# Two graph layers on one core: a PSUM bank for each matching tile, one power per tile, small steps back on VectorE, and the first gathers spaced by a GpSimd step

## The chip, the cores and the metric

The kernel runs on one core of a Trainium2 chip. The metric is the device time of one execution in microseconds (us); less is better. The kernel before took 754.28 us, the median of 14 runs (747.26 to 760.17).

## What is computed

`x` is 4096 x 512 and `adj` is 4096 x 4096, both float32. About 0.2% of `adj` is not zero, and the diagonal is always there, so a row has about nine entries. Cut to what matters:

```python
# layer 0
a = adj + eye;  d = a.sum(1) ** -0.5
x = layernorm(x + relu((d[:, None] * a * d[None, :]) @ x @ W.T + b))
# layer 1: eight heads, masked so hard that each row attends to itself alone
x = layernorm(x + einsum(softmax(q k^T / 8 + 0.01 eye - 1e16 (1 - adj)), x @ Wv, Wo))
```

Off the diagonal an entry of `adj` is below one, so the mask leaves every row only itself; layer 1 is then a product with one 512 x 512 matrix, `wvo`. The kernel tests that this holds and goes to a general version (`general`) where it doesn't. With the given data that version is not run.

## The kernel before

**Tiles.** There are 32 row tiles of 128 rows. In `order`, twelve tiles come first, then the five that stay in SBUF, then the rest, which are loaded a second time.

**First phase** (about 0 to 220 us of the profile). All of `adj` is read once. ScalarE sums rows, TensorE computes `y = d * (x @ W.T)`, which goes to DRAM. VectorE already sorts out entries: for each row tile, `extraction` takes the eight largest of every 512 columns with `max` and `max_index` (L731, L732), sixteen long instructions a tile, and packs value and column into `rec` with some twenty-five short ones.

**Second phase** (from about 220 us to the end). For every tile `i` the loop runs `k` from 0 to 9. At each `k` it emits, in this order and for all engines together, one matmul with a 128 x 128 selection matrix `s_t` against a gathered tile `g` (L1265), one gather 18 ahead (`gather`, L1057, an indirect DMA issued by GpSimd; 19 buffers), one build of a later `s_t` by ScalarE (`spread`, L955 to L968), and a share of VectorE's extraction. Ten such products make one tile of layer 0. The rest of a tile's way is spread over the next three tiles' steps by the table `at`: T transposes the result `h` on TensorE and copies it to `hT` (L668), M multiplies by `wvo` (`times`, L675), Q takes squares on ScalarE, V adds them on VectorE, the power -1/2 is taken by GpSimd (`power`, L1164), and F scales and stores on ScalarE (`finish`, L1170). An entry (2, 6) means: at step 6 of the tile that comes two later. `near` is the table of the last two tiles, `far` that of the others. `scaled` and `residual` (L1126, L1137, VectorE) come at step 1 of the next tile, `eps_var` (L1151, ScalarE) at its step 6.

**Matching.** Rows have different numbers of entries, so rows are paired and long ones hand entries to short ones. This is a chain of six stages per tile, each called at a fixed step: KEY (ScalarE, L808) from the row counts `n_all`; ACROSS (TensorE, L815) transposes the key into PSUM; RANKS (ScalarE, L822) reads that; PERM (VectorE, L832); MOVE (TensorE, L840 and L843) writes merged entries to PSUM; END (VectorE, L851 to L854, and ScalarE, L856) reads them into `wr_all` and `cols_all`. Both PSUM results lie in one bank, the tile `bank`: `pk` in columns 0 to 127, `merged` behind it.

**Order.** [...] An instruction that waits holds everything behind it on its engine. [...]

Of the kernel before, what the change touches and what calls it, by code (L numbers as in the profile page):

```python
# [9 lines left out]
FP = mybir.dt.float32  # L10
# [409 lines left out]
def few_edges_below_one(  # L420
# [46 lines left out]
    ps_a = ctx.enter_context(tc.tile_pool(name="ps_a", bufs=5, space=bass.MemoryType.PSUM))  # L467
    first = ExitStack()
    p1 = first.enter_context(tc.tile_pool(name="first", bufs=2))

# [239 lines left out]
    def extraction(t, a_t, rec):  # L710

        v = v_all[:, t, :]
        vu = v.bitcast(U32)
        idx = keys.tile([P, C], U32, name="idx")
        key = keys.tile([P, 2, C], U32, name="key")
        keyf = key.bitcast(FP)
        top = keys.tile([P, 2, K], FP, name="top")  # L720
        topu = top.bitcast(U32)
        own = keys.tile([P, E], FP, name="own")
        mask = keys.tile([P, C], FP, name="mask")
        ints = keys.tile([P, 2, K], U32, name="ints")
        w = rec[:, 1]
        home = slice(t // TS * E, (t // TS + 1) * E)
        long = []
        for s in range(SEGS):
            o = slice(s * E, (s + 1) * E)
            seg = a_t[:, ts(s, SW)]  # L730
            long.append(lambda o=o, seg=seg: nc.vector.max(v[:, o], seg))  # L731
            long.append(lambda o=o, seg=seg: nc.vector.max_index(idx[:, o], v[:, o], seg))  # L732

        def stt(out, a, sc, b, op0, op1, **kw):
            return lambda: nc.vector.scalar_tensor_tensor(out, a, sc, b, op0=op0, op1=op1, **kw)

        def both(a):
            return a.rearrange("p (o c) -> p o c", o=1).to_broadcast([P, 2, a.shape[1]])

        def one(out, a, s1, s2, **kw):  # L740
            return lambda: nc.vector.tensor_scalar(out, a, s1, s2, **kw)

        def top8(f, r):
            return lambda: nc.vector.max(top[:, f, r * 8 : r * 8 + 8], keyf[:, f])  # L744
# [6 lines left out]
        short = [  # L751
            [

                stt(own, idx[:, home], spot[:, t % TS : t % TS + 1], v[:, home],
                    ALU.is_equal, ALU.mult, accum_out=own_all[:, t : t + 1]),
                stt(key[:, 0], idx, 12, place[:, 0], ALU.logical_shift_left, ALU.bitwise_or),
            ],
            [
                stt(key[:, 1], vu, 0x7FFFF, place[:, 1], ALU.bitwise_and, ALU.bitwise_or),
                stt(key[:, 0], vu, 19, key[:, 0], ALU.logical_shift_right, ALU.bitwise_or),  # L760
            ],
            [stt(keyf, both(v), 0.0, keyf, ALU.is_gt, ALU.mult)],
            [stt(keyf[:, :, home], both(own), 0.0, keyf[:, :, home], ALU.is_equal, ALU.mult)],
            [
                top8(1, 0),
                lambda: nc.scalar.activation(
                    mask, keyf[:, 0], AF.Sign, accum_out=n_all[:, t : t + 1]
                ) if second else nc.vector.tensor_scalar(
                    mask, keyf[:, 0], 0.0, 0.0, op0=ALU.is_gt, op1=ALU.add,
                    accum_out=n_all[:, t : t + 1],  # L770
                ),
            ],
            [drop(1, 0), top8(0, 0)],
            [top8(1, 1), drop(0, 0)],
            [drop(1, 1), top8(0, 1)],
            [top8(1, 2), drop(0, 1)],
            [top8(0, 2)],
            [
                one(ints[:, 1], topu[:, 0], 0xFFF, 19, op0=ALU.bitwise_and,
                    op1=ALU.logical_shift_left),  # L780
                one(ints[:, 0], topu[:, 0], 12, 0xFFF, op0=ALU.logical_shift_right,
                    op1=ALU.bitwise_and),
            ],
            [
                stt(w.bitcast(U32), topu[:, 1], 0x7FFFF, ints[:, 1],
                    ALU.bitwise_and, ALU.bitwise_or),
                lambda: nc.vector.tensor_copy(rec[:, 0], ints[:, 0]),
            ],
            [one(rec[:, 2], w, 0.0, row1n, op0=ALU.is_gt, op1=ALU.mult)],
            [lambda: nc.vector.tensor_tensor(  # L790
                rec[:, 3:6], rec[:, 0:3], upper(rec)[:, 0:3], ALU.subtract
            )],
            [lambda: nc.vector.tensor_tensor(
                rec[:, 6], rec[:, 4], upper(rec)[:, 4], ALU.subtract
            )],
        ]
        return long, short


    bank = ps_t.tile([P, 512], FP, name="bank", bufs=1)  # L800
    second = []

    def match_key(t):
# [7 lines left out]
        return key  # L811

    def match_across(key):
        pk = bank[:, :P]
        tc.keep_in_program_order(nc.tensor.transpose(pk, key.to_broadcast([P, P]), ident))  # L815
        return pk

# [17 lines left out]
    def match_move(rec, perm):  # L835

        r = upper(rec)
        merged = bank[:, P : P + 7 * KH].rearrange("p (f k) -> p f k", f=7)
        tc.keep_in_program_order(
            nc.tensor.matmul(merged, perm[:, 0], r[:, :, :KH], start=True, stop=False)  # L840
        )
# [7 lines left out]
    def match_end(t, merged):  # L849
# [2 lines left out]
        nc.vector.tensor_tensor(wr[:, 0:3], wr[:, 0:3], merged[:, 3:6], ALU.add)  # L852
        nc.vector.tensor_tensor(wr[:, 1], wr[:, 1], merged[:, 6], ALU.add)  # L853
        nc.vector.tensor_scalar(cols_all[:, t], wr[:, 0], float(N - 1), None, op0=ALU.min)  # L854
        if second:
            nc.scalar.activation(wr[:, 3], wr[:, 1], AF.Copy, scale=-1.0)  # L856
        else:
            nc.vector.tensor_scalar(wr[:, 3], wr[:, 1], -1.0, None, op0=ALU.mult)

# [186 lines left out]
    mat = ctx.enter_context(tc.tile_pool(name="mats", bufs=3))  # L1046
    AHEAD = 18

    SUMMED = (NT - 2, NT - 1)
    slots = {}  # L1050

    def gather(j):
        if j >= NT * KH:
            return
        t, k = order[j // KH], j % KH
        slots[j] = p2.tile([P, D], FP, name="g", bufs=AHEAD + 1)
        nc.gpsimd.indirect_dma_start(  # L1057
            out=slots[j], out_offset=None, in_=y[:, :],
# [52 lines left out]
    def own_part(i):  # L1111
        t = order[i]
        own = own_all[:, t : t + 1]
        d = d_all[:, t : t + 1]
        nc.scalar.activation(own, own, AF.Identity, scale=d, bias=d)  # L1115

    def own_bias(i):
        own = own_all[:, order[i] : order[i] + 1]
# [10 lines left out]
        )  # L1129

    def residual(i, c=slice(0, D), part=0):
        if i % 2 == 0 and i not in sts:
            sts[i] = small.tile([P, 2, 5], FP, name="sums")
            sts[i + 1] = sts[i][:, 1]
            pairs[i] = sts[i]
            sts[i] = sts[i][:, 0]
        nc.vector.scalar_tensor_tensor(  # L1137
            hs[i][:, c], hs[i][:, c], 0.0, xs[i][:, c], op0=ALU.max, op1=ALU.add,
            accum_out=sts[i][:, part : part + 1],
# [17 lines left out]
            st[:, 3:4], st[:, 3:4], LN_EPS * LN_EPS, st[:, 1:2], op0=ALU.add, op1=ALU.add  # L1157
        )

    def power(i, n):  # L1160

        j = i % 2
        st = pairs[i - j][:, j : j + n]
        nc.gpsimd.tensor_tensor(  # L1164
            st[:, :, 4], st[:, :, 3], mhalf.to_broadcast([P, n]) if n > 1 else mhalf, ALU.pow
        )

    def finish(i):
        r_t = p2.tile([P, D], FP, name="r_t")
# [36 lines left out]
    yo, zs, hs, pts, hTs, ws, sts, pairs, mats, halves = ({} for _ in range(10))  # L1206
# [11 lines left out]
    shares = iter(was + (n + 1) * (count[1] - was) // (SPREAD * KH) for n in range(SPREAD * KH))  # L1218


    def at(step, i, k):

        near = {"T": (1, 5), "M": (1, 8), "Q": (2, 2), "V": (2, 3), "F": (2, 7)}
        far = {"T": (2, 0), "M": (2, 6), "Q": (3, 1), "V": (3, 4), "F": (3, 8)}
        for table, tiles in ((near, range(NT - 2, NT)), (far, range(NT - 2))):
            behind, place = table[step]
            if k == place and i - behind in tiles:
                return i - behind
        return None

    for i in range(NT + 2):
        if i < NT:
# [3 lines left out]
        has_p = 0 <= p < NT  # L1236
        for k in range(KH):
            ends = p == NT - 1
            t = at("T", i, k)
            if t not in (None, NT - 1):  # L1240
                hTs[t] = evacuate(p2, "hT", transpose_rows(hs[t]))
            t = at("M", i, k)
            if t not in (None, NT - 1):
                ws[t] = times(hTs.pop(t), wvo)
            if i == NT - 1:

# [43 lines left out]
                load_own(i + 2)  # L1290
            if k == 3 and i + 1 < NT:
                own_part(i + 1)
            t = at("Q", i, k)
            if t is not None:
                squares(ws[t], D**-0.5, sts[t][:, 3:4])

            t = at("V", i, k)
            if t is not None:
                variance(t)
                if t >= NT - 2:  # L1300
                    power(t, 1)
                elif t % 2:
                    power(t - 1, 2)
            if k == 6 and i < NT:
                own_bias(i)
            if k == 6 and has_p:
                eps_var(p)
            t = at("F", i, k)
            if t is not None and (t >= NT - 2 or t % 2):
                if t < NT - 2:  # L1310
                    finish(t - 1)
# [43 lines left out]
```

## Time and profile before

| | us |
|---|---|
| median of 14 runs | 754.28 |
| the profiled execution, its own time | 759.6 |
| its span, first to last instruction | 757.7 |
| TensorE busy (matmul) | 600.5 |
| VectorE busy | 546.1 |
| ScalarE busy | 525.3 |
| GpSimd busy | 395.1 |

The profiled execution took 759.6 us, of which 757.7 is the span and 1.9 lies around it. It is 5.3 us (0.7%) over the median. Busy times are shares of one execution; matmuls overlap, so a busy TensorE is not one at its peak. In the waits, "A <- B" says that A stood idle until B released it, "issue" that the profile shows no reason, and "remote" that the releaser isn't in the profile. The granted clock is the share of full speed that TensorE got.

### The profile page before, as it was taken

The numbers are of one execution on the slowest core, as the hardware profiler recorded it, in microseconds if no ns is written. First come the engines' busy times: TensorE is split into PE (matmuls) and PEld (weight loads), VectorE is DVE, ScalarE is ACT, GpSimd is POOL, SyncE is SP. The second block draws the span as 40 slices with busy tenths as digits, with TensorE's granted clock in tenths as the row PEclk, the third lists the DMA queues.
The fourth block names the chain that finished last, engine by engine and source line by source line (L and its number), as shares of the span: only waits on it lengthen the run. The fifth ranks groups of instructions, "written<-read, shape, count | busy, mean of one in ns | idle before, by whom it ended". The sixth has DMA issues, their size and how long they took to land. (4 is left out here: it accounts for less than half of the span.)

```text
span 757.7 us, 8023 instructions
## 1 busy us (share of the span) xinstructions
PE 600.5 (79%) x1638; PEld 276.8 (37%) x1638; DVE 546.1 (72%) x2109; ACT 525.3 (69%) x1152; POOL 395.1 (52%) x494
## 2 busy tenths in 40 slices
PE   1799969877816489689888899988977789798592
PEld 0444434333302134244434344433433344343251
DVE  6679989999996298879969999787884343323310
ACT  2787697858875378579868698777853978775222
POOL 3223223322347566667665676675755566767500
PEclk9999989999967789799999999999998799999887
DMA  9999999999947599999998899987986567678501
GB/s 344 403 422 422 422 428 401 424 422 380 422 174 258 169 361 361 327 357 352 389 337 305 296 321 324 367 282 254 357 296 203 171 210 258 213 225 252 186 14 61
DMA packets 54411, 230.54 MB, mean 304 GB/s; under 512 B 8592, under 2 KB 9616, under 8 KB 48080
## 3 DMA queue, kind: packets, MB, share of 16 engines
q1 hardware_dynamic: 18416, 119.55, 40.0%
q0 software_dynamic: 30800, 100.95, 39.1%
q10 hardware_dynamic: 5136, 9.44, 3.3%
q14 instruction: 44, 0.36, 0.1%
q8 instruction: 15, 0.25, 0.1%
HBM read 213.12 MB, written 16.78 MB: 303 GB/s over the span
## 5 line engine op out<-in xcount | busy, mean ns | idle before, releaser
L1057 POOL DMA_INDIRECT g<-y,cols_all x320 | 314.4, 982 | 147.8 <-issue 77.5
L1265 PE MATMUL acc<-g,s_t 128*128 128x512 f32 x600 | 286.5, 624 | 20.0 <-DMA yo<-y 19.3
L731 DVE MAX8 v_all<-a_t 128x8 f32<-128x512 f32 x256 | 169.2, 681 | 17.1 <-DMA a_t<-in_adj_dram 17.1
L732 DVE FIND_INDEX8 idx<-v_all,a_t 128x8 uint32<-128x512 f32 x256 | 174.3, 685 | 0.0
L1265 PEld LDWEIGHTS acc<-g,s_t 128*128 128x128 f32 x600 | 116.3, 201 | 153.5 <-issue 151.0
L675 PE MATMUL acc<-wvo,hT 128*128 128x512 f32 x256 | 130.9, 653 | 28.5 <-ACT hT L668 11.8
L675 PE MATMUL acc<-wT,xT 128*128 128x512 f32 x256 | 123.6, 630 | 16.2 <-ACT xT L668 11.9
L687 ACT ACTIVATE dump<-a_t 128x2048 uint8<-128x2048 f32 (+1 forms) x52 | 119.5, 2298 | 0.8 <-ACT s_t L968 0.8
L675 PEld LDWEIGHTS acc<-wvo,hT 128*128 128x128 f32 x256 | 52.0, 210 | 93.9 <-issue 70.5
L675 PEld LDWEIGHTS acc<-wT,xT 128*128 128x128 f32 x256 | 49.2, 201 | 73.1 <-issue 52.2
L959 ACT ACTIVATE s_t<-sq,wr_all 128x128 f32<-128x128 f32 x160 | 71.9, 484 | 0.3 <-ACT sq L955 0.3
L955 ACT ACTIVATE sq<-cols,wr_all 128x128 f32<-128x128 f32 x192 | 67.0, 392 | 6.6 <-DVE wr_all L851 4.1
L968 ACT ACTIVATE s_t<-s_t,wr_all 128x128 f32<-128x128 f32 x150 | 52.3, 390 | 4.4 <-ACT r_t L1170 2.5
L682 ACT ACTIVATE dump<-a_n 128x4096 uint8<-128x4096 f32 x15 | 54.4, 3630 | 0.3 <-DMA a_n<-in_adj_dram 0.3
L744 DVE MAX8 top<-key 128x8 f32<-128x64 f32 x192 | 39.4, 216 | 19.2 <-remote 14.0
L856 ACT ACTIVATE wr_all<-wr_all 128x10 f32<-128x10 f32 x24 | 5.0, 208 | 57.1 <-DVE wr_all L853 32.0
L694 POOL TENSOR_SCALAR deg<-deg_all 128x1 f32<-128x1 f32 x32 | 6.9, 234 | 64.4 <-ACT dump L682 64.3
L540 POOL DMA_DIRECT2D x_t<-in_x_dram x32 | 18.0, 566 | 42.1 <-PE pt L663 41.7
L1119 DVE SCALAR_TENSOR_TENSOR yo<-yo,own_all,b_bc 128x512 f32<-128x512 f32 x32 | 23.8, 744 | 21.9 <-ACT own_all L1115 8.7
L704 POOL DMA_DIRECT2D y<-y_t x32 | 19.0, 594 | 37.4 <-ACT y_t L702 36.8
L1164 POOL TENSOR_TENSOR sums<-sums,mhalf 128x2 f32<-128x2 f32 (+1 forms) x17 | 12.4, 727 | 49.6 <-DVE sums L1156 45.0
L702 ACT ACTIVATE y_t<-acc,d_all 128x512 f32<-128x512 f32 x32 | 21.5, 686 | 23.1 <-POOL d_all L697 17.8
(123 smaller groups left out, 668.0 us busy)
## 6 DMA issues: line engine op xcount, KB each, us to landing
a_t<-in_adj_dram SPq DMA_DIRECT2D x30, 2048.0 KB
a_n<-in_adj_dram SPq DMA_DIRECT2D x15, 2048.0 KB
x_t<-in_x_dram POOLq DMA_DIRECT2D x32, 256.0 KB
y<-y_t POOLq DMA_DIRECT2D x32, 256.0 KB
yo<-y SPq DMA_DIRECT2D x32, 256.0 KB
x_t<-in_x_dram SPq DMA_DIRECT2D x32, 256.0 KB
out_dram<-r_t ACTq DMA_DIRECT2D x32, 256.0 KB
g<-y,cols_all POOLq DMA_INDIRECT x320
```

Of the source, the lines that this page charges most:

```text
L675: nc.tensor.matmul(u, srcT[:, dc, :], w[:, dc, :], start=(dc == 0), stop=(dc == ND - 1))
L682: nc.scalar.activation(dump[:, : part.shape[1]], part, AF.Copy, accum_out=dst)
L687: nc.scalar.activation(dump[:, o], a_t[:, o], AF.Relu, scale=-1.0, accum_out=neg_all[:, t, halves[0] : halves[0] + 1],)
L731: long.append(lambda o=o, seg=seg: nc.vector.max(v[:, o], seg))
L732: long.append(lambda o=o, seg=seg: nc.vector.max_index(idx[:, o], v[:, o], seg))
L744: return lambda: nc.vector.max(top[:, f, r * 8 : r * 8 + 8], keyf[:, f])
L955: nc.scalar.activation(sq, cols1, AF.Square, bias=wr[:, 2, k : k + 1])
L959: nc.scalar.activation(s_t[:, k, :], away(), AF.Relu, scale=wr[:, 3, k : k + 1], bias=wr[:, 1, k : k + 1],)
L968: nc.scalar.activation(s_t[:, k, :], s_t[:, KH, :], AF.Copy, scale=wr[:, 1, k : k + 1])
L1057: nc.gpsimd.indirect_dma_start(out=slots[j], out_offset=None, in_=y[:, :], in_offset=bass.IndirectOffsetOnAxis(ap=cols_all[:, t, k : k + 1 ...
L1119: nc.vector.scalar_tensor_tensor(yo[i], yo[i], own, b_bc, op0=ALU.mult, op1=ALU.add)
L1265: nc.tensor.matmul(zs[i], mats[i][:, k, :], slots.pop(i * KH + k), start=(k == 0), stop=(k == KH - 1),)
```

## The change

- **PSUM.** `bank` becomes two tiles, `pk` and `pm`, of a bank each. `acc` gets four banks in place of five.
- **From ScalarE to VectorE**, in the second phase: the count of a row's entries (`n_all`, L766), the negated weights at the end of END (L856), and `own_part` (L1115). KEY and RANKS stay on ScalarE.
- **Powers.** `power` and `finish` are called for each tile, not for pairs of tiles; the sums get a tile of 128 x 5 each.
- **Steps.** The copy to `hT` gets a step E of its own, three steps behind the transposes; `eps_var` gets a step S, ten steps behind `residual` in place of five; M, Q, V and F move by one or two steps. The matching is called in another order and at other steps.
- **Spacing.** Ahead of each of the gathers 4 to 39, GpSimd adds one to a 128 x 100 constant and writes it to a tile that nothing reads.

```diff
-    ps_a = ... tile_pool(name="ps_a", bufs=5, PSUM)
+    ps_a = ... tile_pool(name="ps_a", bufs=4, PSUM)
...
-                lambda: nc.scalar.activation(mask, keyf[:, 0], AF.Sign, accum_out=n_all[:, t : t + 1])
-                if second else nc.vector.tensor_scalar(mask, keyf[:, 0], 0.0, 0.0, ...),
+                one(mask, keyf[:, 0], 0.0, 0.0, op0=ALU.is_gt, op1=ALU.add, accum_out=n_all[:, t : t + 1]),
...
-    bank = ps_t.tile([P, 512], FP, name="bank", bufs=1)
-        pk = bank[:, :P]
+        pk = ps_t.tile([P, 512], FP, name="pk", bufs=1)[:, :P]
-        merged = bank[:, P : P + 7 * KH].rearrange("p (f k) -> p f k", f=7)
+        pm = ps_t.tile([P, 512], FP, name="pm", bufs=1)
+        merged = pm[:, : 7 * KH].rearrange("p (f k) -> p f k", f=7)
...
-        if second:
-            nc.scalar.activation(wr[:, 3], wr[:, 1], AF.Copy, scale=-1.0)
-        else:
-            nc.vector.tensor_scalar(wr[:, 3], wr[:, 1], -1.0, None, op0=ALU.mult)
+        nc.vector.tensor_scalar(wr[:, 3], wr[:, 1], -1.0, None, op0=ALU.mult)
...
+    SPACED = range(4, 4 * KH)
+    space = p2.tile([P, 100], FP, name="space", bufs=1)
...
+        if j in SPACED:
+            nc.gpsimd.tensor_scalar(space, cols1[:, :100], 1.0, None, op0=ALU.add)
         slots[j] = p2.tile([P, D], FP, name="g", bufs=AHEAD + 1)
         nc.gpsimd.indirect_dma_start(...)
...
-        nc.scalar.activation(own, own, AF.Identity, scale=d, bias=d)
+        nc.vector.tensor_scalar(own, own, 1.0, d_all[:, t : t + 1], op0=ALU.add, op1=ALU.mult)
...
-    def power(i, n):        # n = 2: a pair of tiles
+    def power(i):
+        st = sts[i]
+        nc.gpsimd.tensor_tensor(st[:, 4:5], st[:, 3:4], mhalf, ALU.pow)
...
-        near = {"T": (1, 5), "M": (1, 8), "Q": (2, 2), "V": (2, 3), "F": (2, 7)}
-        far = {"T": (2, 0), "M": (2, 6), "Q": (3, 1), "V": (3, 4), "F": (3, 8)}
+        near = {"T": (1, 5), "E": (1, 5), "M": (1, 8), "S": (1, 6), "Q": (2, 2), "V": (2, 3), "F": (2, 7)}
+        far = {"T": (2, 0), "E": (2, 3), "M": (2, 7), "S": (2, 1), "Q": (3, 0), "V": (3, 3), "F": (3, 6)}
...
-                match(*{1: (RANKS,), 3: (MOVE, PERM), 6: (END,), 7: (KEY,), 9: (ACROSS,)}.get(k, ()))
+                match(*{2: (RANKS,), 4: (MOVE,), 5: (PERM, KEY), 8: (ACROSS, END)}.get(k, ()))
```

More of the change, by code (lines that the diff above doesn't have):

```diff
@@ L466, in few_edges_below_one @@
     ps_t = ctx.enter_context(tc.tile_pool(name="ps_t", bufs=2, space=bass.MemoryType.PSUM))
-    ps_a = ctx.enter_context(tc.tile_pool(name="ps_a", bufs=5, space=bass.MemoryType.PSUM))
+    ps_a = ctx.enter_context(tc.tile_pool(name="ps_a", bufs=4, space=bass.MemoryType.PSUM))
     first = ExitStack()
@@ L765, in extraction @@
                 top8(1, 0),
[L766 to L771, printed above, removed]
+                one(mask, keyf[:, 0], 0.0, 0.0, op0=ALU.is_gt, op1=ALU.add,
+                    accum_out=n_all[:, t : t + 1]),
             ],
@@ L1113, in own_part @@
         own = own_all[:, t : t + 1]
-        d = d_all[:, t : t + 1]
-        nc.scalar.activation(own, own, AF.Identity, scale=d, bias=d)
+        nc.vector.tensor_scalar(own, own, 1.0, d_all[:, t : t + 1], op0=ALU.add, op1=ALU.mult)
     def own_bias(i):
@@ L1131, in residual @@
     def residual(i, c=slice(0, D), part=0):
[L1132 to L1136, printed above, removed]
+        if i not in sts:
+            sts[i] = small.tile([P, 5], FP, name="sums")
         nc.vector.scalar_tensor_tensor(
@@ L1158, in variance @@
         )
-    def power(i, n):
[L1162 to L1166, printed above, removed]
+    def power(i):
+        st = sts[i]
+        nc.gpsimd.tensor_tensor(st[:, 4:5], st[:, 3:4], mhalf, ALU.pow)
     def finish(i):
@@ L1204, in test @@
         nc.vector.tensor_scalar(bad, both[0:1, :], -1.0, 1.0, op0=ALU.mult, op1=ALU.add)
-    yo, zs, hs, pts, hTs, ws, sts, pairs, mats, halves = ({} for _ in range(10))
+    yo, zs, hs, pts, hTs, ws, sts, mats, halves = ({} for _ in range(9))
     to_build = iter(
@@ L1218, in few_edges_below_one, with at @@
     shares = iter(was + (n + 1) * (count[1] - was) // (SPREAD * KH) for n in range(SPREAD * KH))
-    def at(step, i, k):
-        near = {"T": (1, 5), "M": (1, 8), "Q": (2, 2), "V": (2, 3), "F": (2, 7)}
-        far = {"T": (2, 0), "M": (2, 6), "Q": (3, 1), "V": (3, 4), "F": (3, 8)}
+    def at(step, i, k, end=NT):
+        found = []
+        near = {"T": (1, 5), "E": (1, 5), "M": (1, 8), "S": (1, 6), "Q": (2, 2), "V": (2, 3), "F": (2, 7)}
+        far = {"T": (2, 0), "E": (2, 3), "M": (2, 7), "S": (2, 1), "Q": (3, 0), "V": (3, 3), "F": (3, 6)}
         for table, tiles in ((near, range(NT - 2, NT)), (far, range(NT - 2))):
             behind, place = table[step]
-            if k == place and i - behind in tiles:
-                return i - behind
-        return None
+            if k == place and i - behind in tiles and i - behind < end:
+                found.append(i - behind)
+        return found
     for i in range(NT + 2):
@@ L1238, in few_edges_below_one @@
             ends = p == NT - 1
[L1239 to L1243, printed above, removed]
+            for t in at("T", i, k, NT - 1):
+                pts[t] = transpose_rows(hs[t])
+            for t in at("E", i, k, NT - 1):
+                hTs[t] = evacuate(p2, "hT", pts.pop(t))
+            for t in at("M", i, k, NT - 1):
                 ws[t] = times(hTs.pop(t), wvo)
@@ L1292, in few_edges_below_one @@
                 own_part(i + 1)
-            t = at("Q", i, k)
-            if t is not None:
+            for t in at("Q", i, k):
                 squares(ws[t], D**-0.5, sts[t][:, 3:4])
-            t = at("V", i, k)
-            if t is not None:
+            for t in at("V", i, k):
                 variance(t)
[L1300 to L1303, printed above, removed]
+                power(t)
             if k == 6 and i < NT:
                 own_bias(i)
[L1306 to L1311, printed above, removed]
+            for t in at("S", i, k):
+                eps_var(t)
+            for t in at("F", i, k):
                 finish(t)
```

## The prediction

> **What bounds the kernel now.** I read the page first, then the busy time by windows, the groups of the second phase, and the order of time on VectorE, GpSimd and TensorE. The windows come first (start and end, length, then busy time and count of each engine, clock, DMA share):
>
> ```profile
> 240.00:260.00 20.00, 11.71 (x28) 4.74 (x26) 4.78 (x16) 5.10 (x13) 14.29 (x16) 0.93 0.68 207
> 300.00:320.00 20.00, 12.56 (x25) 4.90 (x25) 15.89 (x58) 11.56 (x33) 13.14 (x14) 0.74 0.92 314
> 340.00:360.00 20.00, 19.39 (x54) 8.66 (x53) 20.00 (x78) 18.23 (x49) 15.11 (x16) 1.00 0.97 349
> 230.00:565.00 335.00, 286.00 (x742) 128.12 (x743) 274.75 (x993) 243.42 (x675) 221.23 (x228) 0.92 0.89 317
> 565.00:745.00 180.00, 151.12 (x400) 69.35 (x398) 61.64 (x244) 110.10 (x308) 100.18 (x106) 0.92 0.61 193
> ```
>
> Where nothing disturbs (340 to 360) TensorE is busy 19.39 of 20 us and a tile takes about 13 us. The 21 tiles from 230 to 565 took 16 us each. TensorE was busy for 437.1 us of the 515 us of phase two; the other 78 us are waits, and they are what this change can reach. From 240 to 260 only GpSimd is at work: VectorE has 4.78 us of work, ScalarE 5.10. VectorE there:
>
> ```profile
> 244.13 0.95 POOL L1057 DMA_INDIRECT g<-y,cols_all  x1 [0.30 <-DMA g<-y,cols_all]
> 246.63 0.94 POOL L1057 DMA_INDIRECT g<-y,cols_all  x1 [0.30 <-issue]
> 248.10 0.17 DVE L735 SCALAR_TENSOR_TENSOR key<-own,key 128x16 f32<-128x16 f32 x1 [3.44 <-issue]
> 252.31 0.23 DVE L744 MAX8 top<-key 128x8 f32<-128x64 f32 x1 [3.42 <-remote]
> 260.69 0.23 DVE L744 MAX8 top<-key 128x8 f32<-128x64 f32 x1 [4.57 <-remote]
> 264.04 0.48 PE L815 MATMUL bank<-ident,rank_key 128*128 128x128 f32 x1 [9.80 <-ACT above L822]
> 281.04 0.95 POOL L1057 DMA_INDIRECT g<-y,cols_all  x1 [0.30 <-issue]
> 295.40 3.60 PE L1265 MATMUL acc<-g,s_t 128*128 128x512 f32 x8
> ```
>
> Each of these instructions is as short as elsewhere; what grows is the wait ahead of it, and VectorE waits for its own earlier instruction. GpSimd meanwhile issues 27 gathers without a break, one per 1.25 us (0.95 and a gap of 0.30). Such waits add up to 50.8 us between 224 and 590, and to 0.6 us between 30 and 224, where there are no gathers. TensorE, in order, ends up behind L815. The groups from 230 us on:
>
> ```profile
> L815 PE MATMUL bank<-ident,rank_key 128*128 128x128 f32 x23 | 7.1, 308 | 32.3 <-DVE wr_all L853 11.3 <-ACT above L822 9.8 <-DVE v_all L731 3.0
> L675 PE MATMUL acc<-wvo,hT 128*128 128x512 f32 x256 | 130.9, 653 | 28.5 <-ACT hT L668 11.8 <-issue 11.6 <-ACT rank_key L808 4.4
> L856 ACT ACTIVATE wr_all<-wr_all 128x10 f32<-128x10 f32 x24 | 5.0, 208 | 57.1 <-DVE wr_all L853 32.0 <-DVE idx L732 8.7 <-DVE v_all L731 6.1
> L1164 POOL TENSOR_TENSOR sums<-sums,mhalf 128x2 f32<-128x2 f32 x15 | 11.2, 750 | 40.2 <-DVE sums L1156 35.5 <-DVE rec L741 3.1 <-issue 1.3
> ```
>
> L815 and L675 hold 60.8 us of TensorE's 78.
>
> **The change part by part**, against the profiled execution (759.6 us: span 757.7, 1.9 around it; 5.3 over the median of 754.28).
>
> *A bank each.* ACROSS (L815, step 9) overwrites the tile that END (step 6) reads, so TensorE stands behind VectorE's L853: 11.3 us in four waits. With two tiles it waits only for its key and the last RANKS; END and the next MOVE are six steps apart. What is late next is T, which waits for `h` from VectorE: 3.5 us now (L663). I take 11.3 - 3.5 = -7.8; bounds 0 and 32.3 - 9.8 = 22.5 (the 9.8 belongs to the spacing). One `acc` bank less costs nothing: a buffer is needed again after four allocations, which is two tiles, while a product tile is freed at step 1 of the next and the `wvo` tile 9 steps after M. If that cover were gone, TensorE would wait for F, about two steps or 2.6 us a tile.
>
> *To VectorE.* ScalarE loses 24 x 0.208 (L856) + 18 x (0.244 + 0.191) (L766) + 31 x 0.380 (L1115) = 24.6 us of work, and the 57.1 us for which L856 held it. Behind L856 stand the builds, the copy to `hT` and KEY, for which TensorE waits 11.8 + 4.4; 5.1 of that is the last tile's, which keeps its steps. Of the other 11.1 I take half, -5.5; bounds 0 and 11.1. VectorE gains about 24 x 0.157 (as L853) + 18 x 0.29 (the first phase's form) + 31 x 0.206 (as L1156) = 15.4 us. It no longer waits for ScalarE's `own_part` (8.7) and mask (8.1), which would pay for it, but not in full windows: 4 of the 17 between 230 and 565 have VectorE at 19.9 of 20 or more. 4/17 of 15.4 is +3.6; bounds -1.4 and 15.4.
>
> *Steps.* `eps_var` moves to ten steps behind `residual`, so ScalarE's 17.7 us behind L1137 go; Q has three steps after M in place of five, so its 12.9 us on TensorE may grow. By count of the stages, END comes one to five tiles ahead of its gathers in both versions. I take 0; bounds -5 and +5, that difference of 4.8 either way.
>
> *Powers.* 32 x 0.558 against 15 x 0.750 + 2 x 0.558 is 5.5 us more on GpSimd, and 15 more gaps of 0.30: 10.0. Gathers queue behind them, and for gathers `gather` runs 18 x 1.25 = 22 us ahead, so 0 on the path; without that cover, 10.0.
>
> *Spacing.* The trace has no such step. A 128x1 tensor_scalar on GpSimd took 0.234 us, the 128x128 select 0.284; an instruction behind a gather started 0.03 us after it. I take 0.30 a step, 36 x 0.30 = 10.8 us on GpSimd, and little else is queued there. The first forty gathers are consumed as they land (3.2 us after their start), so this is on the path: number 4 starts at 227.85 as now, number 40 at 227.85 + 36 x 1.55 = 283.7 in place of 281.04, and it lands at 286.9. Tile 3 could then end at 287.5; it ended at 299.0 (295.40 + 3.60). So if the breaks let VectorE go on, -11.5; if they don't, +2.6. A second stall at 305 to 312 (7.2 us on L675) could go too, so the bounds are -18.7 and +2.6. I take -11.5, since VectorE is slow only within unbroken runs of gathers.
>
> [...]
>
> After the 9.80 wait fourteen halves of products took 8.31 us from 266.61, against 6.17 from 323.13 at full clock. [...]
>
> *Sum.* -7.8 - 5.5 + 3.6 - 11.5 = -21.2: 738.4 against the profiled 759.6, and 733.1 on the scale of the median.
>
> **Rivals.** *The spacing does nothing* (VectorE's slow waits have another cause), the rest works: 754.3 - 7.8 - 5.5 + 3.6 = 744.6. For it: later slow stretches (390 to 397, 545 to 553) also come in runs of only 9 to 11 gathers.
>
> *VectorE takes all back*: no gain from spacing, and 15.4 us wholly on the path: 754.3 - 13.3 + 15.4 = 756.4. For it: VectorE is at 274.75 of 335, and 50 of the rest is slow waits. Against it: the 16.8 us that it no longer waits for ScalarE.
>
> *Slower: powers hold the gathers.* Every power now waits in GpSimd's queue for its own variance, and the spaced gathers have used up the lead. Gathers alone would end at 223.95 + 320 x 1.25 + 10.8 + 32 x 0.86 = 662; the last ends now at 712.8, and 33 us follow. Up to the last gather L1164 waited 18.8 us for L1156, four times, 4.7 each. From 50 us of such waits on GpSimd sets the end. If 16 of 32 wait, 75 us: 662 + 75 + 33 + 1.9 = 772 profiled, 767 as a median. Against it: four of 17 waited, which scaled to 32 is 35 us.
>
> **How the numbers follow.** Forecast 0.42 (733), spacing idle 0.20 (745), VectorE 0.14 (756), powers 0.24 (767). About 0.5% (3.8 us) is what a measurement can tell from no change; so faster 0.62, same 0.14, slower 0.24. The range goes from 714, near the sum with the larger bounds of the bank and the spacing (-22.5 - 5.5 + 3.6 - 18.7 = -43.1, 711), to 767, where the slower case stands.
>
> **What would show it.** Right: between 240 and 260 VectorE is busy 12 us or more; L815 no longer waits for L853, and its idle time falls from 32.3 to under 15; L668 and L808 release L675 for under 10 us; tile 3 ends by 290. Wrong: VectorE's waits for itself stay near 50 us, or only move behind gather 40; L1164 waits over 50 us before the last gather, and L1265 then waits for `g`.

## The result and the profile after

The changed kernel took 769.57 us (median of 10 runs) against 752.92 us for the kernel before (47 runs beside them): 1.0219, with a 95% interval of 1.0184 to 1.0254. It is 16.7 us slower where the forecast was 21.2 us faster. The profiled execution took 772.44 us, its span 770.6. One thing is needed to read the numbers below: in some comparisons the kernel before ran at about 750 us and in others at about 710, so each kernel is held only against the runs of the kernel before that were made beside it.

The windows of the changed kernel (start and end, length, then busy time and count of TensorE, its weight loads, VectorE, ScalarE, GpSimd, then granted clock, DMA share, GB/s):

```profile
240.00:260.00 20.00, 11.80 (x28) 4.16 (x27) 14.23 (x57) 18.22 (x48) 17.71 (x24) 0.84 0.70 243
300.00:320.00 20.00, 12.48 (x32) 5.30 (x30) 7.28 (x31) 4.50 (x10) 13.85 (x15) 0.91 0.84 285
340.00:360.00 20.00, 19.34 (x49) 8.83 (x50) 19.87 (x87) 18.91 (x48) 14.70 (x16) 0.91 0.94 349
230.00:565.00 335.00, 269.07 (x690) 118.25 (x691) 257.33 (x1020) 228.77 (x598) 234.86 (x263) 0.89 0.85 303
565.00:745.00 180.00, 154.41 (x418) 70.18 (x417) 82.77 (x303) 113.07 (x299) 116.18 (x123) 0.95 0.70 226
```

From 240 to 260 VectorE now does 14.23 us of work in place of 4.78, as forecast, and TensorE still only 11.80. From 230 to 565 TensorE does 269.07 us where it did 286.00, VectorE 257.33 where it did 274.75: both lost 17 us. What is left over is done after 565.

The order of time after, from GpSimd, TensorE and ScalarE (lines left out are marked):

```profile
231.07 0.99 POOL L1055 DMA_INDIRECT g<-y,cols_all  x1 [0.30 <-issue]
...
234.62 0.50 POOL L1053 TENSOR_SCALAR space<-cols 128x100 f32<-128x100 f32 x1
235.29 1.02 POOL L1055 DMA_INDIRECT g<-y,cols_all  x1 [0.17 <-issue]
...
236.31 2.04 PE L1256 MATMUL acc<-g,s_t 128*128 128x512 f32 x2 [14.97 <-DMA x_t<-in_x_dram]
236.32 0.49 POOL L1053 TENSOR_SCALAR space<-cols 128x100 f32<-128x100 f32 x1
236.99 1.01 POOL L1055 DMA_INDIRECT g<-y,cols_all  x1 [0.17 <-issue]
...
315.35 0.69 ACT L1160 ACTIVATE r_t<-acc,sums 128x512 f32<-128x512 f32 x1 [17.53 <-POOL sums L1156]
...
323.33 5.29 PE L675 MATMUL acc<-wvo,hT 128*128 128x512 f32 x8 [7.79 <-ACT hT L668]
```

Three things stand here. From one gather to the next it is 1.70 us (236.99 less 235.29; 1.69 on most), not 1.55. The first product starts at 236.31, where before it started at 229.78. And the scaled store L1160 holds ScalarE for 17.53 us for a power that stands behind a gather, while TensorE waits 7.79 us for the copy to `hT` behind it. The products of tile 3 ended at 308.2 us; before, at 299.0.

The groups from 230 to 745 us:

```profile
L810 PE MATMUL pk<-ident,rank_key 128*128 128x128 f32 x23 | 6.3, 273 | 0.0
L675 PE MATMUL acc<-wvo,hT 128*128 128x512 f32 x238 | 125.8, 677 | 57.5 <-ACT hT L668 32.2 <-issue 9.8 <-ACT above L817 8.0
L1160 ACT ACTIVATE r_t<-acc,sums 128x512 f32<-128x512 f32 x29 | 19.8, 684 | 93.2 <-POOL sums L1156 76.8 <-issue 16.4
L1156 POOL TENSOR_TENSOR sums<-sums,mhalf 128x1 f32<-128x1 f32 x29 | 17.2, 593 | 51.1 <-DVE sums L1150 27.5 <-DVE ints L741 12.1 <-DVE bad L1194 7.7
```

ACROSS (L810, L815 before) lost all its 32.3 us of waits, and L675 gained 29.0. The waits of the same stretch that are new:

```profile
DVE yo L1116 <- DMA yo<-y: 28.6, 13, 4.4
PE acc L1256 <- DMA g<-y,cols_all: 18.0, 8, 6.2
```

TensorE had no wait for `g` of this kind before; `own_bias` (L1116) waited 6.0 us in all for the rows of `y` before.

### The profile page after: what moved, and what is told of

The parts are those of the page before. It is cut to its first block, busy times and chain, and to the rows that moved or that the text cites. A ratio compares the mean times of both kernels' runs of the same rounds, so it can differ in the third digit from the quotient of the medians.

```text
span 770.6 us, 8055 instructions
## 1 busy us (share of the span) xinstructions
PE 599.6 (78%) x1638; PEld 274.4 (36%) x1638; DVE 551.5 (72%) x2201; ACT 512.9 (67%) x1060; POOL 421.0 (55%) x545
## 5 line engine op out<-in xcount | busy, mean ns | idle before, releaser
L731 DVE MAX8 v_all<-a_t 128x8 f32<-128x512 f32 x256 | 172.0, 681 | 16.3 <-DMA a_t<-in_adj_dram 16.2
L675 PE MATMUL acc<-wvo,hT 128*128 128x512 f32 x256 | 133.9, 672 | 58.1 <-ACT hT L668 32.2
L1256 PEld LDWEIGHTS acc<-g,s_t 128*128 128x128 f32 x600 | 110.7, 196 | 155.7 <-issue 118.4
L675 PE MATMUL acc<-wT,xT 128*128 128x512 f32 x256 | 125.0, 638 | 26.2 <-ACT xT L668 17.1
L675 PEld LDWEIGHTS acc<-wvo,hT 128*128 128x128 f32 x256 | 53.9, 217 | 135.6 <-issue 76.9
L1160 ACT ACTIVATE r_t<-acc,sums 128x512 f32<-128x512 f32 x32 | 21.9, 684 | 95.7 <-POOL sums L1156 79.2
L675 PEld LDWEIGHTS acc<-wT,xT 128*128 128x128 f32 x256 | 50.1, 204 | 85.8 <-issue 54.7
L1156 POOL TENSOR_TENSOR sums<-sums,mhalf 128x1 f32<-128x1 f32 x32 | 18.8, 588 | 67.4 <-DVE sums L1150 43.7
L1123 DVE SCALAR_TENSOR_TENSOR h<-acc,d_all,yo 128x512 f32<-128x512 f32 (+1 forms) x33 | 23.9, 724 | 39.0 <-PE acc L1256 27.1
L1116 DVE SCALAR_TENSOR_TENSOR yo<-yo,own_all,b_bc 128x512 f32<-128x512 f32 x32 | 23.9, 745 | 35.8 <-DMA yo<-y 28.6
L961 ACT ACTIVATE s_t<-s_t,wr_all 128x128 f32<-128x128 f32 x150 | 48.2, 391 | 0.9 <-issue 0.2
L744 DVE MAX8 top<-key 128x8 f32<-128x64 f32 x192 | 40.3, 215 | 10.4 <-remote 7.9
```

The lines of the kernel that those rows point to most:

```text
L675: nc.tensor.matmul(u, srcT[:, dc, :], w[:, dc, :], start=(dc == 0), stop=(dc == ND - 1))
L961: nc.scalar.activation(s_t[:, k, :], s_t[:, KH, :], AF.Copy, scale=wr[:, 1, k : k + 1])
L1116: nc.vector.scalar_tensor_tensor(yo[i], yo[i], own, b_bc, op0=ALU.mult, op1=ALU.add)
L1256: nc.tensor.matmul(zs[i], mats[i][:, k, :], slots.pop(i * KH + k), start=(k == 0), stop=(k == KH - 1),)
```

## Experiments

### The spacing

e1 is the changed kernel without the step, e10 the same beside other runs; e9 is the changed kernel once more, beside e10. e5 is the kernel before with a step of 76 columns, e7 the changed kernel with a step of one column.

```diff
 e1, e10 (from after)
-        if j in SPACED:
-            nc.gpsimd.tensor_scalar(space, cols1[:, :100], 1.0, None, op0=ALU.add)
 e5 (from before)
+        if j in SPACED:
+            nc.gpsimd.tensor_scalar(space, cols1[:, :76], 1.0, None, op0=ALU.add)
 e7 (from after)
-            nc.gpsimd.tensor_scalar(space, cols1[:, :100], 1.0, None, op0=ALU.add)
+            nc.gpsimd.tensor_scalar(space[:, :1], cols1[:, :1], 1.0, None, op0=ALU.add)
```

> The changed kernel without the GpSimd step ahead of gathers 4 to 39. Theory C (ScalarE stands at the scaled store, L1160, until GpSimd, which issues its gathers late, takes the power; the copies to hT and the keys stand behind it, and TensorE waits for them): the first such wait (17.5 us) goes since gather 51 is issued about 16 us earlier, the later ones (62 us) stay because the powers are still three steps ahead of their use; 762 us. Theory S (the spacing itself is what costs, 36 steps of 0.44 us at the front of the path): 769.6 - 16 = 754 us or less. In both VectorE's slow waits for itself should be back between 10 and 40 us after the first gather.

> The kernel before with the spacing alone (128x76 in place of 128x100, for want of SBUF). Theory S (the spacing paces the first seven tiles by GpSimd's gathers, whatever stands behind them): what it costs here is what taking it away gave back in the changed kernel, 1.4%, so 760 to 764 us against 753; VectorE's slow waits early in the phase are gone and L1265 waits for g. Theory T (the spacing only hurts where single powers stand in the same queue): within 0.5% of 753, or less, since the early stall is cured.

> The changed kernel with a spacing step of 128x1 in place of 128x100. Theory S: only the length of the step matters; it was 0.49 us and made a gather's period 1.69 us in place of 1.25; at 0.23 us the period is about 1.45 and 45% of the 10.5 us stays: 757 to 761 us. Its rival (the break between gathers, however short, is what costs): 765 to 770 us.

> The changed kernel as it is, to have it beside the next ones on one chip. If VectorE's slow waits belong to the chip, as the last runs say (0.6 to 1.7 us in total there against 20 to 50), the ratio depends on the chip: 1.022 on one with slow waits, 1.03 on one without. Theory S+P+C (spacing 1.2 to 1.4%, fifth acc bank 0.6 to 1%, single powers and later steps the rest) holds on both.

> The changed kernel without the spacing, beside it. Theory S: 1.2 to 1.4% faster than the changed kernel, on either kind of chip. Rival (the spacing cures a stall that only some chips have): no difference on a chip with slow waits, 1.2% on one without.

| | us | before beside it | ratio (95%) |
|---|---|---|---|
| e1 | 753.53 | 748.85 | 1.0079 (1.0028 to 1.0129) |
| e5 | 719.03 | 711.67 | 1.0116 (1.0076 to 1.0156) |
| e7 | 732.15 | 711.67 | 1.0312 (1.0247 to 1.0376) |
| e9 | 742.07 | 710.41 | 1.0426 (1.0392 to 1.0461) |
| e10 | 729.40 | 710.41 | 1.0256 (1.0217 to 1.0295) |

The step costs 12.7 us between e9 and e10, 7.4 us alone in e5, and 1.4% between e1 and the changed kernel (there across two comparisons). It gains nothing in any of them, and e9's 1.0426 is more than the 1.03 that was expected.

Does it end the stall that it was meant for? The work of VectorE from 240 to 260 us tells. In the comparisons where the kernel before ran at about 750 us ("at 750 us" from here on), it is 3.13 to 5.59 us in all seven traces without the step (the kernel before, e1, e2, e13 to e16) and 13.93 to 14.23 in all three with it (the changed kernel, e3, e4). In the others ("at 710 us"), it is 10.54 to 14.33 in all ten traces, with the step or without. First e1, then e12 (below), neither with a step:

```profile
240.00:260.00 20.00, 17.76 (x41) 6.78 (x39) 5.14 (x25) 8.18 (x20) 15.12 (x17) 0.92 0.70 213
```

```profile
240.00:260.00 20.00, 13.05 (x27) 4.82 (x26) 10.83 (x38) 11.38 (x32) 13.38 (x14) 0.74 0.90 308
```

In e1 the first 28 gathers follow each other unbroken until 265.55. VectorE stands meanwhile at `scaled` of tile 0 until 269.28, though the tile's products ended at 249, and ScalarE at RANKS until 264.39. With the step, `scaled` of tile 0 comes at once. The waits of e1, then the line of the changed kernel:

```profile
DVE h L1120 <- remote: 18.1, 1, 18.1
ACT above L817 <- remote: 16.2, 1, 16.2
```

```profile
248.74 0.73 DVE L1123 SCALAR_TENSOR_TENSOR h<-acc,d_all,yo 128x512 f32<-128x512 f32 x1
```

So the step does end the early stall where there is one. Unbroken gathers alone don't make it, since in e12 the first 25 follow each other unbroken too; what else it takes is open. VectorE's waits for its own earlier instruction show a part of it only. From the first gather to the end they sum to 52.5 us before, 33.8 in e1 and 36.2 in the changed kernel, where the first over 0.4 us comes at 328, behind gather 40; in e10 and e12 they sum to 0.6 and 1.6.

Why the cure gains nothing is read from the traces; no run takes it apart. e1 and the changed kernel start their first product together (236.15 and 236.31). Gather 40 then starts at 285.10 in e1 and at 296.24 with the step, and up to 312 TensorE waits 18.0 us for `g` with the step, in e1 only ahead of its first product. `scaled` of tile 3 is still ahead with the step, 308.21 against 314.35; that of tile 15 is behind, 515.1 against 509.6. Between them lies the 17.53 us wait for the first power. Of the thirteen traces without the early stall, eleven have such a wait, of 10.7 to 17.5 us (15.4 in e12, with powers in pairs); the other two are e3 and e4, whose edits are aimed at it. In the seven with the stall no wait at that store is over 6.8 us up to 400. In e3, without that wait, VectorE does nothing from 330 to 340: another stall has come behind the spaced gathers.

e7 against e10 is a comparison across two sets of runs, and their intervals overlap: whether a short step costs anything stays open. It costs less than the long one (1.0312 against e9's 1.0426).

### A PSUM bank less for `acc`

The pools of the kernel before ask for eight PSUM banks (two for `pt`, one for `bank`, five for `acc`), those of the changed kernel for eight as well (two for `pt`, one each for `pk` and `pm`, four for `acc`). e2 takes the fifth `acc` bank from the kernel before. e14 takes it in the first phase only. e8 is the changed kernel without spacing and with one bank for the matching again (five for `acc`). e12 is the kernel before with the banks cut for each phase: five and one shared in the first, four and one each in the second.

```diff
 e2:  ps_a bufs=5 -> 4
 e14: first phase  ps_a bufs=5 -> 4;  second phase  ps_a bufs=5
 e8 (from e1):
-    ps_a ... bufs=4        -> bufs=5
-        pk = ps_t.tile(... name="pk");  pm = ps_t.tile(... name="pm")
+        pk = bank[:, :P];  merged = bank[:, P : P + 7 * KH]
 e12 (from before):
+    first phase:  ps_a bufs=5, bank
+    second phase: ps_a bufs=4, pk, pm
```

> The kernel before with four acc banks in place of five, one bank left unused, nothing else. Theory P (the fifth bank was needed in the first phase): the first gather starts 4 to 7 us later and the time is 757 to 760 us against 753. Theory C gives the first phase no part: 753 us. In the second phase the powers in pairs keep two wvo tiles, so TensorE may also wait for L1170 here; then it is more than 760.

> The changed kernel without the spacing, and with one shared bank and five acc banks as before; the steps, the single powers and VectorE's added work stay. Theory P (the fifth acc bank is worth 4 to 5 us in the first phase, and two banks for the matching little): the first gather starts 4 to 6 us earlier and the time is 746 to 750 us. Its rival (two banks are worth the 7.8 us that was forecast, and make up for the lost acc bank): 754 to 760 us, with L815 waiting for VectorE again.

> The kernel before with five acc banks and the shared bank in the first phase, and with four acc banks and a bank each for pk and pm in the second; the steps stay. As forecast for the banks alone: 7.8 us or 1% faster, with L815 no longer waiting for L853. Rival (L815's wait only moves to the next instruction of TensorE that needs VectorE or ScalarE): within 0.5%. Theory P: the first product no later than in the kernel before.

> The kernel before with four acc banks in the first phase and five in the second. Theory P (the first phase needs the fifth bank: TensorE waits for ScalarE's y_t): 0.6 to 1.2% slower, the first product 4 to 8 us later, the rest as before. Rival (the acc bank is missed in the second phase): within 0.4%.

| | us | before beside it | ratio (95%) | first product at |
|---|---|---|---|---|
| e2 | 754.20 | 748.85 | 1.0060 (1.0013 to 1.0106) | 234.2 |
| e8 | 718.25 | 711.67 | 1.0128 (1.0045 to 1.0211) | 228.0 |
| e12 | 707.69 | 710.41 | 0.9967 (0.9939 to 0.9995) | 228.8 |
| e14 | 758.54 | 756.43 | 1.0049 (1.0001 to 1.0098) | 236.8 |

Five banks in the first phase start the second at 228 to 230 us (at 232 in e11 and e17, below), four at 234 to 237. The waits of TensorE in the first phase (20 to 236 us), in e14 and then in the kernel before of the same comparison (e13):

```profile
PE acc L675 <- ACT xT L668: 15.8, 10, 8.7
PE acc L675 <- ACT y_t L702: 9.3, 5, 3.2
```

```profile
PE acc L675 <- ACT xT L668: 12.3, 11, 4.6
PE acc L675 <- ACT y_t L702: 5.4, 5, 2.2
```

`acc` holds `x @ W.T` there until ScalarE has copied it to `y_t`: with four banks TensorE waits 3.9 us more for that and 3.5 us more for `xT`, and everything after it starts later, the first gather too. This holds in all traces: the wait for `y_t` is 7.8 to 10.4 us in the ten with four banks and 3.8 to 5.9 in the ten with five. In the second phase the fifth bank isn't missed: e12 gives it to the matching there and is 2.7 us faster, by 0.3% the only version here whose interval stays below no change. The 7.8 us that were expected of the banks alone it does not show, and e14's 0.5% is a little under the 0.6 that was expected.

### ScalarE's wait for the power

e3 lets the scaled store take the variance, which is ready earlier, in place of its power -1/2, so that the output's scale differs and nothing waits for a power. e4 moves the changed kernel's F six steps later; e6 does so without spacing.

```diff
 e3 (from after)
-        nc.scalar.activation(r_t, ws.pop(i), AF.Copy, scale=sts.pop(i)[:, 4:5])
+        nc.scalar.activation(r_t, ws.pop(i), AF.Copy, scale=sts.pop(i)[:, 3:4])
 e4 (from after), e6 (from e1)
-        far = {..., "F": (3, 6)}
+        far = {..., "F": (4, 2)}
```

> The changed kernel, where the scaled store takes the variance in place of its power -1/2: the power is still taken by GpSimd, but nothing waits for it, so the output's scale is another. All instructions are the same. Theory C: ScalarE's 79 us of waits for L1156 go, L675's idle time falls from 58 to under 30 us, and the time to 750 to 756 us. Theories S and P: no change, 768 to 771 us.

> The changed kernel with the scaled store F of all but the last two tiles at step 2 of the tile four later, nine steps behind the power in place of three; nothing else. Theory C: as with no wait at all, 750 to 757 us, unless TensorE then waits for the acc bank (reused five steps later). Theories S and P: 768 to 771 us.

> The changed kernel without the spacing and with F at step 2 of the tile four later. Theory C, narrowed (ScalarE's 90 us at L1160 in the run without spacing delay the copies to hT once the gathers are not what ends last): L675's idle time falls from 41 to about 25 us and the time by 5 to 10 us to 744 to 749. Its rival (ScalarE's waits are time that it would have spent idle elsewhere): 752 to 755 us, as without spacing alone.

e3 took 766.32 us, 1.0240 (1.0152 to 1.0327); e4 765.36, 1.0243 (1.0156 to 1.0330); e6 724.44, 1.0183 (1.0109 to 1.0256). The 76.8 us for which ScalarE stood at L1160 look like the loss, and they are not: e3 and e4, in which 0 and 5.5 us of them are left, are as slow as the changed kernel (1.0219), to within 0.9%. In e3 the store waits for the sum instead, and TensorE still waits for the copy behind it and for gathers:

```profile
ACT r_t L1160 <- DVE sums L1150: 46.1, 13, 6.6
...
PE acc L675 <- ACT hT L668: 21.2, 7, 6.1
PE acc L1256 <- DMA g<-y,cols_all: 18.7, 10, 6.6
```

The theory that this wait is the cost fell for the changed kernel. Without the spacing it was not tested: in e6 ScalarE still waits 69.3 us for the power at the store, against 88.9 in e10. Its 1.0183 fits neither time that was expected, and lies under e10's 1.0256 with intervals that overlap.

### The moves to VectorE

e11 is the kernel before with the three moves alone, e15 with `own_part` alone; e13 is the kernel before itself beside e15. e16 is the kernel before with the changed steps, the powers per tile and the banks of e12.

```diff
 e15 (from before); e11: this, and the count and the negation
-        nc.scalar.activation(own, own, AF.Identity, scale=d, bias=d)
+        nc.vector.tensor_scalar(own, own, 1.0, d_all[:, t : t + 1], op0=ALU.add, op1=ALU.mult)
 e16 (from after): without spacing and moves, banks as in e12
```

> The kernel before with the three small steps on VectorE in place of ScalarE, nothing else. As forecast, -5.5 and +3.6 us: within 0.5% of before. Theory V (VectorE is what bounds the tiles with extraction): 0.5 to 1.5% slower, and the last extraction later than in the kernel before.

> The kernel before as it is, for a trace beside the next ones. If VectorE's slow waits come with the state of the machine and not with runs of gathers, they add up to less than 2 us in this trace where the median is near 710, and to more than 20 where it is near 750; gathers still come in unbroken runs of ten to twenty-seven.

> The kernel before with own_part alone on VectorE (31 steps of about 0.2 us). Theory V (VectorE's time counts in full while it extracts): all three moves cost 1.0%, own_part is 6 of their 15 us, so 0.4% slower. Rival (one of the moved steps holds VectorE's order up, not its length): no difference here, or nearly all of the 1.0%.

> The kernel before with the changed steps and single powers, and a bank each in the second phase alone; no spacing, no moves, five acc banks in the first phase. What is left of the change. Theory S+P+V: within 0.5% of before, since nothing of what costs is in it. Theory C (single powers, three steps ahead of their use, hold ScalarE and so TensorE): 0.5 to 1% slower, with L1160's line waiting 80 us for GpSimd.

| | us | before beside it | ratio (95%) |
|---|---|---|---|
| e11 | 719.31 | 710.41 | 1.0103 (1.0068 to 1.0138) |
| e13 | 755.00 | 756.43 | 1.0012 (0.9960 to 1.0064) |
| e15 | 762.09 | 756.43 | 1.0124 (1.0082 to 1.0165) |
| e16 | 753.43 | 756.43 | 0.9967 (0.9905 to 1.0030) |

The moves cost 8.9 us in e11, and `own_part`, 32 instructions of 0.203 us, costs as much by itself in e15 (9.3 us, interval 6.2 to 12.5). Length alone does not explain both: the moved instructions take about 16 us in e11 and 6.5 in e15, although 6.5 is inside e15's interval. The steps and the powers cost nothing that e16 can show, and ScalarE's wait for the power is 26.1 us in it, not 80. The group of `own_bias` in the second phase (222 to 720), in e13 and then in e15:

```profile
L1119 DVE SCALAR_TENSOR_TENSOR yo<-yo,own_all,b_bc 128x512 f32<-128x512 f32 x32 | 23.9, 747 | 20.7 <-ACT own_all L1115 10.0 <-issue 5.6 <-DMA yo<-y 5.1
```

```profile
L1118 DVE SCALAR_TENSOR_TENSOR yo<-yo,own_all,b_bc 128x512 f32<-128x512 f32 x32 | 23.9, 747 | 32.8 <-DMA yo<-y 26.6 <-issue 6.2
```

VectorE stops waiting for ScalarE's `own_part` and waits for the rows of `y` instead. e17 and e18 ask whether that wait is the cost.

```diff
 e17 (from e15), e18 (from e12)
-            if k == 6 and i < NT:
+            if k == (9 if i < NT - 1 else 6) and i < NT:
                 own_bias(i)
```

> The kernel before with own_part on VectorE, as in e15, and own_bias at step 9 of its tile in place of step 6 (the last tile keeps step 6). Theory W (the cost of own_part is a new wait: VectorE gets to own_bias earlier than y's rows have landed and stands behind them, 26.6 us in 13 waits in e15 against 6.0 in two before): the waits L1118 <- DMA yo fall under 10 us and the ratio to before goes from 1.012 back to 1.000 to 1.004. Rival X (VectorE's length: 32 x 0.203 = 6.5 us on an engine that has no break in most windows): the waits fall or not, and the ratio stays at 1.009 to 1.014.

> e12 (two matching banks in the second phase only, five acc banks in the first) with own_bias at step 9; own_part stays on ScalarE. Theory W: the waits of own_bias in e12 were 23.0 us (19.6 for the rows, 3.3 for own_part); without them 0.990 to 0.995 of before, under e12's 0.997. Rival X: those waits are covered, 0.995 to 0.999 as e12.

e17 took 724.50 us against 709.78: 1.0194 (1.0141 to 1.0246). Its waits for `yo` were 37.4 us and did not fall, so both expectations missed. e18 took 709.51: 0.9984 (0.9947 to 1.0020), inside the rival's range, with 16.7 us of such waits, all from tile 23 on.

The traces say why e17 changed so little. `own_bias` and `scaled` of three tiles earlier share a `yo` buffer: `scaled(i-3)` frees it, SyncE then loads tile i's rows, `own_bias(i)` uses them. Tile 19 in e17 and then in e18, in order of time:

```profile
498.46 0.73 DVE L1125 SCALAR_TENSOR_TENSOR h<-acc,d_all,yo 128x512 f32<-128x512 f32 x1
...
499.22 0.33 SPq L1067 DMA_DIRECT2D yo<-y  x1
...
509.71 0.75 DVE L1118 SCALAR_TENSOR_TENSOR yo<-yo,own_all,b_bc 128x512 f32<-128x512 f32 x1 [7.08 <-DMA yo<-y]
```

```profile
487.16 0.73 DVE L1130 SCALAR_TENSOR_TENSOR h<-acc,d_all,yo 128x512 f32<-128x512 f32 x1
487.91 0.33 SPq L1071 DMA_DIRECT2D yo<-y  x1
...
499.71 0.73 DVE L1123 SCALAR_TENSOR_TENSOR yo<-yo,own_all,b_bc 128x512 f32<-128x512 f32 x1
500.36 0.74 DVE L1130 SCALAR_TENSOR_TENSOR h<-acc,d_all,yo 128x512 f32<-128x512 f32 x1
```

The first line is `scaled(16)`, the load and `own_bias(19)` follow. In e18 the load has 11.8 us until `own_bias` and is not waited for. In e17 VectorE reaches `own_bias` 3.4 us after the load's issue and stands still until it lands, 10.5 us after it, with the extraction queued behind. In both, `own_bias(19)` comes ahead of `scaled(17)` (500.36 in e18, 519.2 in e17), although the loops emit `scaled(17)` more than a tile earlier. So the order on an engine is not the order of emission, by which the forecast counted its steps: between the loops and the engine the instructions are dealt anew, and where that is done no run shows. An edit can deal them differently (e12), or leave VectorE's order here as it is (e5, e14). Counted in VectorE's order in the traces (runs of like instructions as one, mean of tiles 10 to 22):

| | instructions from `scaled(i-3)` to `own_bias(i)` | waits of `own_bias` up to tile 22, us | `scaled(10)` to `scaled(21)`, us |
|---|---|---|---|
| e5 | 50 | 0 | 150.7 |
| e12, e18 | 44 | 0, 0 | 153.7, 154.7 |
| e8 (`own_part` on VectorE) | 22 | 15.1 | 166.8 |
| e11 (the same) | 22 | 15.5 | 168.0 |
| e10, e9 (the same) | 23 | 19.5, 20.7 | 172.1, 173.3 |
| e17 (the same) | 20 | 22.3 | 174.1 |
| e13 | 50 | 0 | 170.3 |
| e15 (`own_part` on VectorE) | 16 | 17.2 | 185.9 |

(The last two are from the comparison with the kernel before at 756 us.) With `own_part` on VectorE, `own_bias` is dealt close behind the `scaled` that frees its buffer. VectorE is nearly full in these tiles (147.75 of 160 us from 400 to 560 in e18), so a wait lengthens them: 22.3 us of waits and 19.4 us between e17 and e18. The pair e15 and e13, 17.2 and 15.6, says less. In e15 the profile puts only 11.6 us of the waits down to the rows, and at 750 us the last column does not part the kernels: the kernel before has 176.7 in its own trace, and e1, with `own_part` on VectorE, 172.7. From tile 15 on the first column's counts are the same in e17 as in e15 but for one, so its edit in the source moved nothing there. That the waits are the cost is read from the traces; a kernel with `own_part` on VectorE and `own_bias` dealt later was not run. A part of the cost of e11 and e17 lies ahead of these tiles: their first product comes at 232.2 and 232.6, some 3 us later than in e5, e12 and e18 (228.3 to 229.9). e8, with all the moves, and e15 start as early as those, so why is open.

## Why the prediction was wrong

**Sum.** In the comparison of e9 to e11, where the change cost 31.7 us: spacing 12.7, moves 8.9, the `acc` bank 9.1, give or take 6.5 (e10's 1.0256 less e8's 1.0128, of 710; e8 is from another comparison), and 1.0 is left for the rest. In the comparison of the result it cost 16.7; single runs there give 1.4% (10.5 us) for the spacing, 4.5 for the bank (e2) and 9.3 for `own_part` (1.24% in e15), 24.3 together. So some 8 us are lost only once or given back by the rest; which, no run tells.

**A bank each, -7.8.** The step itself held: L810 waits for nothing. What it is worth stays open. e12 gained 2.7 us and e18 nothing that is clear of noise, but at 710 us the kernels with a shared bank wait at ACROSS for only 0 to 3.4 us in all (e5, e8, e11, e17), so there was little to gain. At 750 us the kernel before waits there for 32.3 and 45.3 us (e13), and only e16 has a bank each with five `acc` banks left to the first phase. It is 2.5 us faster (7.2 faster to 2.3 slower), with the steps and powers in it, and still waits 28.7 us at ACROSS, for ScalarE in place of VectorE. The sentence that failed is "One `acc` bank less costs nothing". It looked at the second phase, where it is true, and forgot that the same pool serves the first, where the bank sets the start: 4 to 9 us.

**To VectorE, -5.5 and +3.6.** Measured +8.9. The waits for ScalarE's `own_part` ended as forecast, but the step that called them a gain asked only who was waited for, not which wait ends last next: as far as the traces tell, the rows of `y`, 28.6 us in the changed kernel. And it took the order from the loops. The rival "VectorE takes all back" had the sign, not the mechanism.

**Steps 0, powers 0.** Held within what e16 can tell (-0.3%, -1.0 to +0.3, with a bank each in it). The 76.8 us of waits at L1160 are not the single powers' doing alone: e12, with powers in pairs, has 51.1, and e16, with a power for each tile, 26.1. e3 shows that in the changed kernel they are not what sets the time.

**Spacing, -11.5.** The largest miss: +12.7 or +7.4, and 1.4% between e1 and the result. Its first half held: the breaks let VectorE go on, and the first forecast sign, 12 us or more from 240 to 260, came true (14.23, against 5.14 in e1 without the step). The step that failed is the one from there to the end, "Tile 3 could then end at 287.5". Gather 40 started at 296.24, not at 283.7: 5.8 us of that is the later start, 6.8 the slower pace. Tile 3 ended at 308.2, with TensorE waiting 18.0 us for `g`; behind it came the wait for the first power, which no trace with the stall has, and stalls of VectorE behind gather 40, a sign that the forecast itself had named as one of being wrong. At 710 us there is no stall to end, and the step only costs. It was also mis-sized: 0.49 us, a shorter gap (0.17 for 0.30) and a gather longer by 0.06 make 0.44 us a gather, 15.8 us for 36, for which 0.30 and 10.8 were taken. With 1.69 in place of 1.55 the forecast's own uncured case, +2.6, comes to +7.7.

**The rivals.** "The spacing does nothing" was wrong for VectorE in the comparison of the result, and had no price for the delay. "Powers hold the gathers" gave 767, near the 769.6 measured, by another way: up to the last gather L1156 waited 43.0 us, under the 50 from which it was to decide, while TensorE did wait 18.0 us for `g`.

**VectorE beside the steps.** Two kinds of its long instructions took as long with the steps as without: from 234 to 300 `h<-h,x_t`, with two inputs, took 679 ns with them (e9) and 675 ns without (e10), and `MAX8` on 512 columns 679 and 680. Of the short ones some took longer: the `CAST` to `rec`, two in each, 332 and 168 ns. What the steps took of GpSimd's own time, 0.44 us a gather, does show. And an instruction that waits holds up what its engine has behind it: in e17's trace the extraction stands behind `own_bias` for 7.08 us.

## What to carry to other kernels

Before a wait is counted as gained, find the next thing that the waiting instruction needs, here a load whose buffer is freed just ahead of it, and read the order from the trace of each engine rather than from the loops. A resource that a pool shares over phases has to be priced in each of them. Ending a stall is worth only what the waits behind it leave, so the next thing that each engine waits for has to be priced along with the remedy. And a stall can be there in one execution of a kernel and absent in another (the changed kernel without the step: VectorE busy for 5.14 us from 240 to 260 in e1, for 13.84 in e10): a remedy has to be priced for both.

## What was not expected of the hardware

VectorE's waits for its own earlier instruction were 52.5 us in one execution and 55.7 in another of the kernel before, and 0.6 to 1.7 in all of e5 to e12, e17 and e18. With all waits over 0.15 us that the profile puts down to VectorE itself, to "issue" or to "remote", it is 51 to 109 us from the first gather on in the ten traces from comparisons at 750 us, and 0 to 0.3 in the ten at 710. One and the same chip gave 748.85 us for the kernel before in one comparison (with e1) and 710.41 in another (with e9). The forecast treated these waits as part of the program. Thirty-six short GpSimd steps between the gathers ended those of the first gathers (VectorE was busy for 14.23 us from 240 to 260, for 4.78 before), and not the later ones (36.2 us in all are left in the changed kernel); what makes them is open.

In the changed kernel's trace a gather behind a step on GpSimd has another pace than one behind a gather: the gap before it is 0.17 us in place of 0.30, and it takes 1.01 to 1.02 us on most in place of 0.95 to 0.99.
